# Last expert layer: router in three units, 14 of 16 experts with slots, the shared products behind the slots

## The chip, the cores and the metric

The kernel runs on one core of one Trainium2 chip. The metric is the device time of one execution in microseconds, from the chip's own clock; four runs of the kernel before give 1216.45, 1203.67, 1218.26 and 1219.77 us, a median of 1217.36 us. A further execution was recorded by the hardware profiler. Engines: PE (TensorE, matrix products), DVE (VectorE), ACT (ScalarE), POOL (GpSimd), SP (SyncE, which here only issues DMAs).

## The reference, cut to what matters

Four layers over 1024 tokens of width 256, each wrapped as `x = x + layernorm(layer(layernorm(x)))`: an attention, an expert layer with 8 experts, a linear attention, and an expert layer with 16 experts. Only the last layer is touched:

```python
scores = softmax(x @ gate_weight.T)                  # 1024 x 16
topk_weight, topk_idx = top_k(scores, 4)
for e in range(16):
    w_e = sum(where(topk_idx == e, topk_weight, 0), -1)
    y = y + w_e[:, None] * glu(x, gate_up_weights[e], down_weights[e])   # 176 hidden channels
y = y + glu(x, shared_gate_up, shared_down)          # 352 hidden channels
glu(x, gu, d) = (silu(x @ g.T) * (x @ u.T)) @ d.T
```

Each token needs 4 of the 16 experts. With the inputs of the reference the experts 0 to 13 get between 231 and 290 tokens each.

## The kernel before, in words

Tokens stand in 8 tiles of 128 (`TT`), in two halves of 4 tiles. `self.hT` holds the normalised input by channel, `self.hrow` by token, and `self.x` the residual. The last layer (`experts1`) splits the hidden channels in two kinds.

**For all tokens ("dense").** The 352 shared channels and those of the experts from `SP1` = 13 on (3 x 176) are 880 hidden channels, or 7 tiles of at most 128 (`tiles`, `group(0)` 4 of them, `group(1)` 3). `gates(i, hf)` makes the gate and up product of one tile for one half of the tokens (4 matmuls of 512 columns each in the profile's counts, `gated`, L821 to L824), and leaves silu(g)*u in `mids[hf]`. Channels of routed experts are then multiplied by the router's share per token (`weighted`, L1667). Those shares come from `spreads`: PE turns the router's weights (L1598), ACT copies them (`wT`, L1599), SP writes them to DRAM (L807) and reads them back spread over the partitions (L1609). `self.down(ps, products(hf), ...)` (L837) is the third product, 7 pieces by 4 token tiles for a half.

**By slots.** For experts 0 to 12 every token row is sent to the expert's region of a DRAM tensor `slots` (room for 336 rows each). `routed(hf)` does it for a half of the tokens in two steps: first the logits `pl` (L1500), softmax, the four best, `counts` (L1505 to L1531); then the places by running counts `pr` (L1538 to L1544), `place` (L1556) and 16 indirect DMAs on POOL's queue (L1562), four for each token tile. A branch on whether an expert overflows (`crowded`, `full`) then picks `to_slots`. It fetches an expert's rows (`xs`, L1704, on SP), turns them (L1711), makes the products (L1690), the third product (L1743), scales by share (`ys`, L1748) and adds the rows into one of two DRAM tensors `sums` with three indirect DMAs on POOL (L1753). The experts' weights come three experts at a time (`sw`, L1459, on SP). Last, `sums` are fetched (L1795), added to the dense part, normalised and stored (`turn_out`).

The order of the work is written out by hand in `experts1` for the dense part and the router; a scheduling layer then orders each engine's queue from that program order by its own estimates, and each engine runs its queue strictly in order. The branch is a border: what stands before it in the program is issued before it on every engine. Before it stand all `gates`, `shifted()` (eight ACT additions to `x`, L314), `weighted(0)`, the third product of the first half, and `weighted(1)`; the third product of the second half stands at the end of `to_slots`. While the router runs, the tile pairs of the layer before are still being normalised and turned (`turning`, L276, L277; `catch_up` releases the pieces).

Of the kernel before, what the change touches and what calls it, by code (L numbers as in the profile page):

```python
# [9 lines left out]
F32, I32, U32 = mybir.dt.float32, mybir.dt.int32, mybir.dt.uint32  # L10
AF = mybir.ActivationFunctionType
# [4 lines left out]
P = 128  # L16
T = 1024
TT = T // P
# [14 lines left out]
FS = 2 * F1  # L33


SP1 = 13
CP, CT = 112, 3
CAP = CP * CT
SLOTS = SP1 * T
SPARE = 16 * T  # L40
FD = FS + (E1 - SP1) * F1
FG1 = 4
L1F = [(lo, min(FG1 * P, FD - lo)) for lo in range(0, FD, FG1 * P)]
FT = F1 - P
UP = 64
# [16 lines left out]
class Net:  # L62
# [240 lines left out]
    def shifted(self):  # L303

        nc = self.nc
        lost = self.small.tile([P, 3, TT], F32, tag="lost", bufs=1, name="lost")
        shift = self.small.tile([P, TT], F32, tag="shift", bufs=1, name="shift")
        nc.gpsimd.tensor_tensor(lost, self.mvs[:, :, :, 0], self.rss, ALU.mult)
        nc.gpsimd.tensor_tensor(shift, lost[:, 0, :], lost[:, 1, :], ALU.add)
        nc.gpsimd.tensor_tensor(shift, shift, lost[:, 2, :], ALU.add)  # L310
        nc.gpsimd.tensor_scalar(shift, shift, -1.0, None, ALU.mult)
        for tt in range(TT):
            x = self.x[:, tt, :]
            self.pinned(nc.scalar.activation(x, x, AF.Identity, bias=shift[:, tt : tt + 1]))  # L314

    def catch_up(self, ps, n):

# [1115 lines left out]
    def experts1(self):  # L1433
        nc, tc, a = self.nc, self.tc, self.a
        with ExitStack() as ctx:
# [45 lines left out]
            nc.gpsimd.memset(within, 1.0)  # L1481
            nc.gpsimd.memset(within[:, :, 0:1], 0.0)
            place = one.tile([P, TT, TOP1], I32, name="place")
            counts = one.tile([P, 2, E1], F32, name="counts")

            def routed(hf):

                n = slice(hf * TT // 2, (hf + 1) * TT // 2)
                N = TT // 2
                sh = [P, N, E1]  # L1490

                def new(name, *shape):
                    return small.tile([P, N, *shape], F32, tag=name, name=name)

                v, c = w[:, n, :], chosen[:, n, :]
                pl = ps.tile(sh, F32, tag="b1", name="pl")
                for i in range(N):
                    for k in range(KC):
                        at = (hf * N + i) * P
                        nc.tensor.matmul(  # L1500
                            pl[:, i, :], self.hT[:, k, at : at + P], wr[:, k, :],
                            start=(k == 0), stop=(k == KC - 1),
                        )
# [9 lines left out]
                for i in range(N):  # L1513
# [15 lines left out]
                )  # L1529
                nc.vector.tensor_tensor(v[:, :, SP1:], v[:, :, SP1:], c[:, :, SP1:], ALU.mult)  # L1530
                nc.vector.tensor_reduce(  # L1531
                    counts[:, hf, :], c.rearrange("p t e -> p e t"), AX.X, ALU.add
                )
                yield


                pr = ps.tile(sh, F32, tag="b1", name="pr")
                nc.tensor.matmul(pr, self.earlier, c, start=True, stop=False)  # L1538
                if hf == 1:
                    nc.tensor.matmul(  # L1540
                        pr, self.ones, counts[:, 0:1, :].to_broadcast(sh), start=False, stop=False
                    )
                for i in range(1, N):
                    nc.tensor.matmul(  # L1544
# [13 lines left out]
                )  # L1558
                for i in range(N):
                    for j in range(TOP1):  # L1560
                        tt = hf * N + i
                        sent = nc.gpsimd.indirect_dma_start(  # L1562
                            out=self.slots[:, :],
                            out_offset=bass.IndirectOffsetOnAxis(
                                ap=place[:, tt, j : j + 1].bitcast(U32), axis=0
                            ),
                            in_=self.hrow[:, tt, :], in_offset=None,
                            bounds_check=SLOTS - 1, oob_is_err=False,
                        )
                        tc.declare_no_dep(sent.ins, group="sent", reason="no two tokens share a slot")  # L1570
                        tc.add_to_no_dep_group("sent", sent.ins)
                yield

            def crowded():

                pc = ps.tile([P, E1], F32, tag="b1", name="pc")
                for hf in range(2):
                    nc.tensor.matmul(pc, self.ones, counts[:, hf, :], start=(hf == 0), stop=(hf == 1))
                most = one.tile([P, 1], F32, name="most")
                nc.vector.tensor_reduce(most, pc[:, 0:SP1], AX.X, ALU.max)  # L1580
                over = one.tile([P, 1], I32, name="over")
                nc.vector.tensor_scalar(over, most, float(CAP), None, ALU.is_gt)
                return nc.values_load(
                    over[0:1, 0:1], min_val=0, max_val=1,
                    skip_runtime_bounds_check_because="the result of a comparison",
                )
# [44 lines left out]
            def gates(i, hf, part=None):  # L1631
                wg, wu, right, m, lo = tiles[i]
                self.gated(ps, tmp, wg, wu, mids[hf][0:m, i, :], m, hf, part)

            quarters = (slice(0, HALF // 2), slice(HALF // 2, HALF))
            first, second = (routed(hf) for hf in range(2))
            early, late = quarters
            gates(0, 0, early)
            gates(1, 0, early)
            self.catch_up(ps, 3)  # L1640
            gates(2, 0, early)
            next(first)
            gates(3, 0, early)
            for i in range(FG1):
                gates(i, 0, late)
            self.catch_up(ps, len(self.todo))
            next(first)
            group(1)
            gates(FG1, 0)
            next(second)  # L1650
            for i in range(FG1 + 1, len(tiles)):
                gates(i, 0)
            gates(0, 1)
            next(second)
            gates(1, 1)
            spreads()
            gates(2, 1)
            full = crowded()
            for i in range(3, len(tiles)):
                gates(i, 1)  # L1660
            self.shifted()

            def weighted(hf):
                for i, (wg, wu, right, m, lo) in enumerate(tiles):
                    if lo in spread:
                        v = mids[hf][0:m, i, :]
                        nc.vector.tensor_tensor(  # L1667
                            v, v, spread[lo][0:m, hf * HALF : (hf + 1) * HALF], ALU.mult
                        )

            def products(hf):
                return [(mids[hf][0:m, i, :], right) for i, (wg, wu, right, m, lo) in enumerate(tiles)]

            weighted(0)
            self.down(ps, products(0), True, 0)
            weighted(1)


            def silu_times(g, pg, pu, mid):
# [19 lines left out]
            def to_slots():  # L1699
# [74 lines left out]
                for e in range(SP1):  # L1774
                    if e + 1 < SP1:
                        turn(e + 1)
                    if e + 3 < SP1:
                        fetch(e + 3)
                    middle(e)
                    if e > 0:  # L1780
                        out(e - 1)
                    if e > 0 and e % S3 == 0 and (e // S3 + 1) * S3 < SP1:
                        load(e // S3 + 1)
                out(SP1 - 1)
# [21 lines left out]
                def plus(dst, x, y):  # L1806
                    nc.vector.tensor_tensor(dst, x, y, ALU.add)

                acc = self.acc
                for tts in pairs[:2]:  # L1810
                    plus(acc[:, tts, :], acc[:, tts, :], other[:, tts, :])
                for tts in pairs[:2]:
                    plus(acc[:, tts, :], acc[:, tts, :], got[:, tts, :])
                    self.turn_out(ps, [tts.start, tts.start + 1])
# [2 lines left out]
                self.down(ps, products(1), True, 1, lambda ps, tts: self.turn_out(ps, tts), other)  # L1817

            def to_all():
                self.down(ps, products(1), True, 1)  # L1820
# [119 lines left out]
```

## Time and profile before

| | us |
|---|---|
| median of four runs | 1217.36 |
| profiled execution, own time | 1224.1 |
| its span, first to last instruction | 1222.3 |
| PE busy / DVE / ACT / POOL in the span | 1126.5 / 706.4 / 514.3 / 220.3 |
| last layer, first gate (1003.3) to the end | 219 |
| of it, dense gates and router, to the end of the last gate (1081.5) | 78.2 |
| slots, first `pe` to last `po` (1101.8 to 1188.4) | 86.6 |
| from there to the end | 33.9 |

Read the profile by stage: the layers before the last are the same instructions in both kernels. In what follows a time such as 1101.8 is in microseconds from the start of the span, and "L1690" is line 1690 of the kernel before. The chain of waits lists, in order of time, what the end of the program is traced back to; the timeline lists one engine's instructions with the idle time before them and what ended it. "Another core or an unknown queue" means that the trace has no instruction that fits the release.

### The profile page before, as it was taken

The numbers are of one execution on the slowest core, as the hardware profiler recorded it, in microseconds if no ns is written. First come the engines' busy times: TensorE is split into PE (matmuls) and PEld (weight loads), VectorE is DVE, ScalarE is ACT, GpSimd is POOL, SyncE is SP. The second block draws the span as 40 slices with busy tenths as digits, with TensorE's granted clock in tenths as the row PEclk, the third lists the DMA queues.
The fourth block names the chain that finished last, engine by engine and source line by source line (L and its number), as shares of the span: only waits on it lengthen the run. The fifth ranks groups of instructions, "written<-read, shape, count | busy, mean of one in ns | idle before, by whom it ended". The sixth has DMA issues, their size and how long they took to land. (4 is left out here: it accounts for less than half of the span.)

```text
span 1222.3 us, 15788 instructions
## 1 busy us (share of the span) xinstructions
PE 1126.5 (92%) x5996; PEld 687.4 (56%) x5996; DVE 706.4 (58%) x1664; ACT 514.3 (42%) x970; POOL 220.3 (18%) x208
## 2 busy tenths in 40 slices
PE   7999999998999999789999999999999889589992
PEld 4543333332547465456767676767676666257672
DVE  5876777760434336677677777777777765033224
ACT  4266666667330102355444444444444434023331
POOL 3100000000100001021111111111111224604662
PEclk9999999999999999899999999999999989879997
DMA  6000000000005111201304131313130211285743
GB/s 204 2 1 1 1 1 1 1 1 1 1 8 182 52 37 50 73 11 58 122 26 128 29 125 30 124 32 106 32 105 35 65 39 37 81 220 136 184 64 113
DMA packets 53495, 76.96 MB, mean 63 GB/s; under 512 B 7226, under 2 KB 44409, under 8 KB 53415
## 3 DMA queue, kind: packets, MB, share of 16 engines
q1 hardware_dynamic: 46886, 68.97, 18.4%
q0 software_dynamic: 6528, 6.93, 3.1%
q8 instruction: 49, 0.80, 0.3%
q14 instruction: 32, 0.25, 0.1%
HBM read 60.88 MB, written 17.00 MB: 64 GB/s over the span
## 5 line engine op out<-in xcount | busy, mean ns | idle before, releaser
L499 DVE TENSOR_REDUCE pm<-sc 128x1 f32<-128x512 f32 x256 | 163.2, 685 | 64.4 <-PE sc L563 43.2
L563 PE MATMUL sc<-qTm,kT 32*128 32x512 f32 x512 | 151.7, 646 | 1.9 <-ACT pe L581 1.9
L592 ACT ACTIVATE pe<-sc 128x512 f32<-128x512 f32 x216 | 117.7, 595 | 67.9 <-PE sc L563 47.3
L1144 ACT ACTIVATE sn<-pt,shift,rs 128x128 f32<-128x128 f32 x256 | 93.7, 470 | 106.9 <-DVE shift L1140 106.9
L494 PE MATMUL sc<-kT,qT 32*128 32x512 f32 x512 | 136.2, 637 | 1.6 <-ACT qT L453 0.8
L1104 PE MATMUL px<-hT,w_l1a 128*128 128x512 f32 x256 | 125.4, 602 | 5.4 <-DVE y L1096 5.1
L1096 DVE SCALAR_TENSOR_TENSOR y<-px,cp,y 128x1023 f32<-128x1023 f32 (+5 forms) x102 | 123.4, 1213 | 4.2 <-ACT y L1090 4.1
L1139 POOL TENSOR_TENSOR rs<-ve,nhalf 128x8 f32<-128x8 f32 x32 | 52.4, 1637 | 304.5 <-DVE ve L1138 249.7
L824 DVE TENSOR_TENSOR mid<-sg,pu 128x512 f32<-128x512 f32 (+2 forms) x50 | 32.0, 642 | 122.1 <-PE pu L821 87.3
L823 ACT ACTIVATE sg<-pg 128x512 f32<-128x512 f32 (+2 forms) x50 | 27.6, 561 | 138.4 <-PE pg L821 122.9
L230 POOL TENSOR_TENSOR rss<-ve,nhalf 128x2 f32<-128x2 f32 x12 | 8.4, 698 | 406.5 <-DVE ve L229 401.7
L550 PE MATMUL po<-pe,va 128*32 128x256 f32 (+1 forms) x872 | 79.2, 431 | 1.3 <-ACT oT L555 0.8
L563 PEld LDWEIGHTS sc<-qTm,kT 32*128 32x128 f32 x512 | 49.6, 185 | 54.0 <-issue 38.3
L1208 PE MATMUL pg<-hT,w_l1a 128*128 128x512 f32 x128 | 62.0, 609 | 9.7 <-DVE og L1324 8.2
L1753 POOL DMA_INDIRECT sums<-ys,number x39 | 56.9, 1459 | 72.5 <-ACT ys L1748 64.2
L550 PEld LDWEIGHTS po<-pe,va 128*32 128x32 f32 x872 | 17.8, 108 | 85.3 <-issue 75.7
L1104 PEld LDWEIGHTS px<-hT,w_l1a 128*128 128x128 f32 x256 | 44.2, 196 | 32.7 <-issue 30.8
L821 PE MATMUL pg<-hT,w_l0f 128*128 128x512 f32 x128 | 62.1, 608 | 0.0
L1174 PE MATMUL pv<-w_l1a,hT 128*128 128x256 f32 x256 | 59.9, 382 | 1.3 <-DVE state L1308 0.7
L1114 ACT ACTIVATE y<-y 128x1024 f32<-128x1024 f32 x32 | 34.2, 1068 | 62.7 <-DVE y L1096 54.2
L821 PE MATMUL pu<-hT,w_l0f 128*128 128x512 f32 x128 | 60.3, 592 | 0.0
L1125 DVE BATCH_NORM_STATS2 st<-pt 128x6 f32<-128x128 f32 x256 | 55.1, 283 | 5.3 <-PE pt L1123 5.3
(275 smaller groups left out, 2041.3 us busy)
## 6 DMA issues: line engine op xcount, KB each, us to landing
spread<-rows SPq DMA_DIRECT2D x32, 512.0 KB
sw<-in_e_s SPq DMA_DIRECT2D x4, 1872.0 KB
slots<-blank SPq DMA_DIRECT2D x13, 357.0 KB
xs<-slots SPq DMA_DIRECT2D x13, 357.0 KB
w<-w SPq DMA_DIRECT2D x9, 512.0 KB
w_l0f<-in_e_wg SPq DMA_DIRECT2D x4, 512.0 KB
w_l0f<-in_e_wu SPq DMA_DIRECT2D x4, 512.0 KB
w_l0f<-in_e_wd SPq DMA_DIRECT2D x4, 512.0 KB
```

The lines of the kernel that those rows point to most:

```text
L494: nc.tensor.matmul(sc, raw[r, tt * P : (tt + 1) * P], kT[r, g, half(kh)], start=True, stop=True,)
L499: nc.vector.tensor_reduce(pm[:, tt, 2 * pair + i, kh : kh + 1], sc, AX.X, ALU.max)
L550: nc.tensor.matmul(po[0][rows(j), c], va[:, st, g * G + j, :], pe[j // 2][:, j % 2, c], start=(st == 0), stop=(st == TT - 1 and c.stop == ...
L563: nc.tensor.matmul(sc, kT[rows(j), g, st * P : (st + 1) * P], qm[rows(j), :], start=True, stop=True,)
L592: nc.scalar.activation(pe[pair][:, i, :], sc, AF.Exp, scale=scale)
L821: nc.tensor.matmul(p, w(k), self.hT[:, k, c], start=(k == 0), stop=(k == KC - 1))
L1096: nc.vector.scalar_tensor_tensor(y[:, at:hi], px[:, at - j : hi - j], column(cw + 4 * h + 3 - j), y[:, at:hi], ALU.mult, ALU.add,)
L1104: nc.tensor.matmul(px[:, c], w[:, k, hh * DK : (hh + 1) * DK], self.hT[:, k, c], start=(k == 0), stop=(k == KC - 1),)
L1144: nc.scalar.activation(sn[:, n, :], pts[n // 4][:, n % 4, :], AF.Identity, scale=rs[:, n : n + 1], bias=shift[:, n : n + 1],)
L1174: nc.tensor.matmul(pv[:, i, :, :].rearrange("p h v -> p (h v)"), self.hT[:, k, (n + i) * P : (n + i + 1) * P], wv[:, k, :], start=(k == 0) ...
L1208: nc.tensor.matmul(pg, wg[:, k, hh * DK : (hh + 1) * DK], self.hT[:, k, c], start=(k == 0), stop=(k == KC - 1),)
L1753: sent = nc.gpsimd.indirect_dma_start(out=self.sums[e % 2][:, :], out_offset=bass.IndirectOffsetOnAxis(ap=number[:, i, :].bitcast(U32), axis=0
```

## The change

Three things change in the last layer. `SP1` goes from 13 to 14, so that the dense hidden channels go from 880 to 704 (6 tiles, the last of 64) and `to_slots` runs over 14 experts. The router works in three units (`UNITS`): token tiles 0 and 1, tiles 2 and 3, tiles 4 to 7; the logits of the first unit stand ahead of all dense gates. `weighted` of both halves, the additions of `shifted` and the third product of the first half move behind the branch: `weighted` and the additions into the first experts of `to_slots`, the third product behind the last expert, where it takes the fetched `sums` as its addend.

```diff
-SP1 = 13
+SP1 = 14
+UNITS = ((0, 2), (2, 2), (4, 4))
@@ shifted
-        for tt in range(TT):
+        def add(tt):
             x = self.x[:, tt, :]
-            self.pinned(nc.scalar.activation(x, x, AF.Identity, bias=shift[:, tt : tt + 1]))
+            nc.scalar.activation(x, x, AF.Identity, bias=shift[:, tt : tt + 1])
+        return add
@@ routed
-            def routed(hf):
-                n = slice(hf * TT // 2, (hf + 1) * TT // 2)
-                N = TT // 2
+            def routed(u):
+                begin, N = UNITS[u]
+                n = slice(begin, begin + N)
...
-                if hf == 1:
+                for i in range(u):
                     nc.tensor.matmul(
-                        pr, self.ones, counts[:, 0:1, :].to_broadcast(sh), start=False, stop=False
+                        pr, self.ones, counts[:, i : i + 1, :].to_broadcast(sh), start=False, stop=False
                     )
@@ order of the work
-            first, second = (routed(hf) for hf in range(2))
+            units = [routed(u) for u in range(len(UNITS))]
             early, late = quarters
+            next(units[0])
             gates(0, 0, early)
+            self.catch_up(ps, 3)
             gates(1, 0, early)
-            self.catch_up(ps, 3)
+            next(units[1])
             gates(2, 0, early)
-            next(first)
+            next(units[0])
             gates(3, 0, early)
-            for i in range(FG1):
+            gates(0, 0, late)
+            next(units[1])
+            for i in range(1, FG1):
                 gates(i, 0, late)
             self.catch_up(ps, len(self.todo))
-            next(first)
             group(1)
             gates(FG1, 0)
-            next(second)
+            next(units[2])
             for i in range(FG1 + 1, len(tiles)):
                 gates(i, 0)
             gates(0, 1)
-            next(second)
+            next(units[2])
             gates(1, 1)
             spreads()
             gates(2, 1)
             full = crowded()
             for i in range(3, len(tiles)):
                 gates(i, 1)
-            self.shifted()
+            shift = self.shifted()
...
-            weighted(0)
-            self.down(ps, products(0), True, 0)
-            weighted(1)
@@ to_slots
                     if e > 0:
                         out(e - 1)
+                    if e in (3, 4):
+                        weighted(e - 3)
+                    if 0 <= e - 3 < TT:
+                        shift(e - 3)
...
                 acc = self.acc
-                for tts in pairs[:2]:
-                    plus(acc[:, tts, :], acc[:, tts, :], other[:, tts, :])
+                self.down(ps, products(0), True, 0, None, other)
                 for tts in pairs[:2]:
                     plus(acc[:, tts, :], acc[:, tts, :], got[:, tts, :])
                     self.turn_out(ps, [tts.start, tts.start + 1])
```

More of the change, by code (lines that the diff above doesn't have):

```diff
@@ L305, in shifted @@
         nc = self.nc
-        lost = self.small.tile([P, 3, TT], F32, tag="lost", bufs=1, name="lost")
-        shift = self.small.tile([P, TT], F32, tag="shift", bufs=1, name="shift")
+        lost = self.route.tile([P, 3, TT], F32, name="lost")
+        shift = self.route.tile([P, TT], F32, name="shift")
         nc.gpsimd.tensor_tensor(lost, self.mvs[:, :, :, 0], self.rss, ALU.mult)
@@ L1483, in experts1 @@
             place = one.tile([P, TT, TOP1], I32, name="place")
-            counts = one.tile([P, 2, E1], F32, name="counts")
-            def routed(hf):
-                n = slice(hf * TT // 2, (hf + 1) * TT // 2)
-                N = TT // 2
+            counts = one.tile([P, len(UNITS), E1], F32, name="counts")
+            def routed(u):
+                begin, N = UNITS[u]
+                n = slice(begin, begin + N)
                 sh = [P, N, E1]
                 def new(name, *shape):
-                    return small.tile([P, N, *shape], F32, tag=name, name=name)
+                    return small.tile([P, TT // 2, *shape], F32, tag=name, name=name)[:, 0:N]
                 v, c = w[:, n, :], chosen[:, n, :]
@@ L1498, in routed @@
                     for k in range(KC):
-                        at = (hf * N + i) * P
+                        at = (begin + i) * P
                         nc.tensor.matmul(
@@ L1531, in routed @@
                 nc.vector.tensor_reduce(
-                    counts[:, hf, :], c.rearrange("p t e -> p e t"), AX.X, ALU.add
+                    counts[:, u, :], c.rearrange("p t e -> p e t"), AX.X, ALU.add
                 )
@@ L1560, in routed @@
                     for j in range(TOP1):
-                        tt = hf * N + i
+                        tt = begin + i
                         sent = nc.gpsimd.indirect_dma_start(
@@ L1576, in crowded @@
                 pc = ps.tile([P, E1], F32, tag="b1", name="pc")
-                for hf in range(2):
-                    nc.tensor.matmul(pc, self.ones, counts[:, hf, :], start=(hf == 0), stop=(hf == 1))
+                for u in range(len(UNITS)):
+                    nc.tensor.matmul(
+                        pc, self.ones, counts[:, u, :], start=(u == 0), stop=(u == len(UNITS) - 1)
+                    )
                 most = one.tile([P, 1], F32, name="most")
@@ L1819, in to_all @@
             def to_all():
-                self.down(ps, products(1), True, 1)
+                for tt in range(TT):
+                    shift(tt)
+                for hf in range(2):
+                    weighted(hf)
+                    self.down(ps, products(hf), True, hf)
                 for e in range(SP1):
```

## The prediction

> **What bounds the kernel now.** Up to 1001 the two kernels run the same instructions, so only the last layer counts. I read its stages first (busy time by stretch), then the chain of waits, then the timelines of POOL, PE and DVE. The stretches show PE full from 1010 to 1050 and from 1101 to 1201, and between them a hole: from 1050 to 1070 PE is busy 5.8 of 20 us, DVE 0.7, ACT 1.2, while POOL works. The chain of waits goes through it:
>
> ```profile
> 1037.35 0.04 ACT sg L823
> 1037.39 14.40 another core or an unknown queue
> ...
> 1052.41 16.95 another core or an unknown queue
> ...
> 1069.38 0.57 ACT wT L1599
> ...
> 1071.40 1.57 DMA w<-wT
> ...
> 1074.34 8.12 DMA w<-w
> ...
> 1082.52 18.76 DMA sw<-in_e_s
> ...
> 1101.81 0.55 PE pe L1690
> ```
>
> Read it as: the router's shares reach ACT at 1069.4, are written and spread by DMA, the experts' rows and weights queue behind them, and the slots start at S = 1101.8. The first 31 us have no owner. By PE's timeline its work was done in time: the turn of the shares (L1598) ends at 1044.4, yet ACT copies it at 1069.4; a gate product ends at 1041.8 and ACT takes it at 1051.8. PE's completions arrive 5 to 25 us late, one in some 8 us, and then all the backlog within 0.4 us at 1070.8. It lies beside POOL's sends:
>
> ```profile
> 1025.38 1.24 POOL L1562 DMA_INDIRECT slots<-hrow,place  x1 [8.97 <-DVE place L1556]
> ...
> 1065.83 0.98 POOL L1562 DMA_INDIRECT slots<-hrow,place  x1 [0.30 <-issue]
> ```
>
> 32 sends, one each 1.28 us, end at 1066.8; the backlog comes 4.0 us later. From 1025 to 1039 they ran without any such delay. The profile shows where it lies, not why. From S on PE sets the pace:
>
> ```profile
> 1088.27 12.02 PE L837 MATMUL po<-w_l1f,mid 112*128 112x256 f32 x44 [0.66 <-DVE mid L1667]
> ...
> 1112.45 3.57 PE L1690 MATMUL pe<-xT,sw 128*128 128x336 f32 x12
> ...
> 1119.03 3.57 PE L1690 MATMUL pe<-xT,sw 128*128 128x336 f32 x12
> ...
> 1188.36 12.27 PE L837 MATMUL po<-w_l1f,mid 128*128 128x256 f32 x56
> ```
>
> One expert takes 1119.03 - 1112.45 = 6.58. The last third products (56) hide behind the last experts' sums, whose fetch lands at 1203.1 to 1205.1; the end is DVE's.
>
> **The change, part by part.** Let S be the start of the slots and compare with 1101.8.
>
> *The extra expert.* +6.58 us of PE from S on. Its three sends on POOL are 3 x 1.76 = 5.3, below 6.58, and its weights ride with the last load (two experts for one): nothing more. Its blank rows are one more DMA of 357 KB in the linear attention, where the DMA share is 1 to 3 tenths: 0.
>
> *The smaller dense part.* 7 tiles to 6. A tile costs 3.43 per half (pg to pg), also at 112 rows, so the gates lose 6.9 us of PE; third products lose 8 of 56 per half, 3.4. This is worth only what S gets from it, counted there. SP issues five spreads for seven, 1.4 MB for 2.2.
>
> *Third product of the first half behind the slots.* PE has 96 matmuls after the last expert for 56: 96 x 0.215 = 20.6, to 1209.0 on the old clock. DVE adds the sums at 1203 or later anyway, and takes the last pair's product at 1211.6 before. So PE stays covered. But DVE's queue comes out otherwise: in the kernel before the pairs of tiles overlap (while one waits for POOL's power, the next pair's statistics run); in the built order after, each pair runs through alone. From rows: addition 0.65, sums 0.65 (two pairs only), statistics 0.75, aggregates 0.2, eps 0.1, POOL 0.85, nb 0.16, then 1.6 to the second `x`. First pair: sums land 1203.1, then 0.65 + 0.75 + 0.2, two additions to `hrow` that wait for later fetches (to about 1207.5), nb and `x`: 1209.2. Second 5.0: 1214.2. Two more of 4.3: 1222.8. Before, the last `x` ends at 1217.3: +5.5; with some overlap left I take +5.0 (bounds 0 and +6).
>
> *Shares and additions behind the branch.* In the built order DVE's eight multiplications (5.5 us) and ACT's additions (7 x 0.41) stand in front of the first rows' copies. They wait for spreads that land before the rows, since both go through SP's queue: 0 while S waits for the weights, up to +5.5 if not.
>
> *PE idles before S.* Its gates end, and nothing is left until the rows land. A row for a cold start: after 1000 the first gate pieces of 256 columns took 1.87, 1.70 and 1.17 for 0.87: 2.1 us lost. I take +2.0 (bounds 0 and 3). Before, the third products stood there and half filled the gap.
>
> *The router in three units.* First sends: PE's logits of unit 0 end near 1004.6, but DVE interleaves its router steps with the last normalisations, ACT needs a table load (1.28) and stands `hT` of the second pair behind the third pair's rows. Counting DVE's rows in the built order, the place of unit 0 comes near 1018 (before: 1024.5), unit 1 near 1024. So the first 16 sends run 1018.7 to 1039.2. In exchange PE waits in its queue for pair two's `hT` (2.0), for `pr` of unit 0 (0.5) and unit 1 (3.0), and starts gates(4) near 1028.5 instead of 1023.2. Then gates 3.43, logits 1.7, gates 3.43, gates 3.43: `pr` of unit 2 at 1040.5 to 1041.7, its place at 1043. POOL has stopped by then; 16 sends take 0.9 + 20.5, to 1064.4. Six us won in front shrink to 2.4 at the end of the sends.
>
> *Sends beside DVE.* The new first burst (1018.7 to 1039.2) overlaps DVE's last normalisations and router steps. The row: from 1024 to 1039 DVE was busy 5.7 of 15 us and the sends kept their 1.28 all the same. So 0; the other bound is 4 sends that take the 1.76 of a sending in the slots: +1.9, inside POOL's pause.
>
> The Trainium skill speaks against it ("SBUF — State Buffer", "SBUF: two separate sides", the box on the "DVE blocks DMA" trap): while DVE runs an operation that takes the port it shares with GpSimd, POOL cannot write descriptors, and a send of 0.62 us takes 3.1. By that rule, as an estimate from the page, five sends beside DVE would each be 2.5 us longer, the first burst would end at 1051 and S come some 8 us later; the pace of 1.28 above shows nothing of it for the operations DVE runs here.
>
> *S.* SP's first `xs` waits for the last send, and the weights stand behind it in SP's queue. Landing +1.0 after the last send (packets of the trace end near 1067.8), then rows and first weights, 2.3 MB at 0.36 MB/us (the best stretch while `sw` runs alone) plus 2.4 for issue and receipt: +8.8. So S = place of unit 2 + 31.2. The other path is the shares: from ACT's copy, 2.9 to the first spread, 1.4 + 2.3 MB at the 0.24 MB/us seen from 1074 to 1092, 18.3 in all. The dense third product, which PE held until 1100.1, isn't in either.
>
> **Sum.** Own time after = 1224.1 + (S - 1101.8) + 6.6 + 5.0 + 2.0 = S + 135.9. Break-even is S = 1088.2. If no completion came late, S = 1043 + 31.2 = 1074.2, 1210.1. If some do in the first 16 sends, and go out while POOL stands still, unit 2's place slips to about 1049 (the first late one cost DVE 4.7 at 1040), the shares get out in the first 14 us of the second burst as at 1025 to 1039, and S = 1080: 1215.9, -8.2. The timed runs have a median of 1217.36, 0.55% below the profiled execution; the same difference there gives **1209**.
>
> **Rivals.** *The hole is back whole*: late completions last to 4 us after the sends, in the second burst too. Place near 1047.7, sends to 1069, shares at 1073.1 to 1074.8, S = 1093.1: +4.9, **1222**. For it: the shares are turned at 1045, inside the second burst. Against: a pause of 4 us or more lets the backlog go. *No late completions*: -14, **1203**. For it: bursts of 16 instead of 32, and 14 us without delay at the start of the old one; against: nothing in the change aims at the cause, which is unknown. *Slower*: the place of unit 2 is the late thing. Three units mean that four results of PE (`pl` and `pr` of units 1 and 2) stand on the path to it instead of two, each 5 to 10 late if completions are late from the first burst on: 1043 + 26 = 1069, S = 1100, +12, **1230**. It is slower at all from a place at 1057 on, and by 1% from 1069. For it: POOL now waits for a place three times, and the old trouble began at 1039 within a microsecond of POOL's long wait for its second place (1038.4 to 1045.9); against: POOL pauses also between units. *It doesn't do what it says* (the first place is no earlier than 1024): no price, since unit 2 decides.
>
> **Chances.** Forecast 0.40 (1203 to 1216), no late completions 0.25 (1199 to 1206), hole back 0.18 (1216 to 1226), slower 0.17 (1226 to 1234). A measurement of this kernel tells about 1% from no change. Below 1205.2 lie most of the second case and a quarter of the first: 0.32; over 1229.5 the last and a little: 0.18; between, 0.50. The range is 1199 to 1228: what is left out is the slow end of the last rival and the tail of the second.
>
> **What would show it.** Right: two bursts of 16 sends with a pause near 1040, `wT` more than 15 us before 1069, first `pe` at 1074 to 1088 ended by `sw` or `xs`, 6.58 per expert, PE done about 21 us after its last `po` of an expert, DVE's last `x` some 34 after it, for 28.9 before. Wrong: releases without an owner after the second burst, a place of unit 2 after 1057, slots that wait for DVE's multiplications, or a tail that PE ends.

## The result

After: median 1216.24 us of 44 runs (1213.30 to 1221.27). Before, now with 70 runs: 1216.02 us (1201.35 to 1225.53). The ratio after to before is 1.0028, 95% interval [1.0014, 1.0042]: 0.3% slower, which lies within the 1% that counts as no change; 1209 was forecast. The ratio leaves out runs over 1.5% above the fastest of their kernel, 21 of before's 70 and none of after's; the profiled execution of before (1224.1) would be one of them. The medians of all runs are 0.2 us apart, so the kernels are equally fast on the whole. The two ranges say more than the medians: before spreads over 24 us, after over 8.

The profiled execution of after took 1217.18 us of its own (span 1215.4). The chain of waits of after, to be read beside that of before:

```profile
1063.01 3.08 PE pg L825 x4
1066.13 0.98 another core or an unknown queue
...
1068.70 2.31 DMA slots<-hrow,place
...
1071.96 8.42 DMA xs<-slots
1080.52 1.35 PE pt L1716 x6
1081.87 5.22 PE pe L1695 x12
```

The 31 us without an owner are one microsecond, and the slots start at S = 1081.7 instead of 1101.8. They now wait for the last send and the fetch behind it. POOL's timeline of after has the two bursts of 16 sends and the pause between them, here the ends of each:

```profile
1017.18 1.24 POOL L1566 DMA_INDIRECT slots<-hrow,place  x1 [2.33 <-DVE place L1560]
...
1036.60 0.97 POOL L1566 DMA_INDIRECT slots<-hrow,place  x1 [0.30 <-issue]
1049.54 0.97 POOL L1566 DMA_INDIRECT slots<-hrow,place  x1 [11.96 <-issue]
...
1068.70 0.97 POOL L1566 DMA_INDIRECT slots<-hrow,place  x1 [0.30 <-issue]
```

Late completions are still there, but cut short; late means that the engine that waits for PE's result goes on well over 0.1 us after PE has ended it. PE's timeline of after at the end of the second burst, and ACT's, which takes these gate products:

```profile
1055.90 1.96 PE L825 MATMUL pg<-hT,w_l1f 128*128 128x512 f32 x4
...
1059.42 1.88 PE L825 MATMUL pg<-hT,w_l1f 128*128 128x512 f32 x4
...
1062.94 1.93 PE L825 MATMUL pg<-hT,w_l1f 128*64 128x512 f32 x4
```

```profile
1058.29 0.60 ACT L827 ACTIVATE sg<-pg 128x512 f32<-128x512 f32 x1 [3.90 <-PE pg L825]
1066.11 0.60 ACT L827 ACTIVATE sg<-pg 128x512 f32<-128x512 f32 x1 [7.23 <-PE pg L825]
1072.47 0.59 ACT L827 ACTIVATE sg<-pg 64x512 f32<-64x512 f32 x1 [5.76 <-remote]
```

The three gate products ended at 1057.9, 1061.3 and 1064.9, so ACT got them 0.4, 4.8 and 7.6 us late, the second with three sends still to go and the third 2.8 us after POOL's end (1069.7). The first burst shows the same from 1030 to 1040: the gate product that ended at 1032.4 was taken at 1040.0.

So the slots gain 20.1 us between the two profiles. What is given back: first product to last third product of the experts 94.3 us for 86.7, and from there to DVE's last sum 34.2 for 28.8. -20.1 + 7.6 + 5.4 and 0.2 at the end is -6.9, the difference of the two profiled executions.

### The profile page after: what moved, and what is told of

Read it like the earlier page. It is cut to its first block, busy times and chain, and to the rows that moved or that the text cites. A ratio compares the mean times of both kernels' runs of the same rounds, so it can differ in the third digit from the quotient of the medians.

```text
span 1215.4 us, 15834 instructions
## 1 busy us (share of the span) xinstructions
PE 1127.6 (93%) x6000; PEld 688.0 (57%) x6000; DVE 706.7 (58%) x1683; ACT 517.2 (43%) x975; POOL 225.0 (19%) x211
## 5 line engine op out<-in xcount | busy, mean ns | idle before, releaser
L1758 POOL DMA_INDIRECT sums<-ys,number x42 | 61.5, 1464 | 52.5 <-ACT ys L1753 43.6
L1118 ACT ACTIVATE y<-y 128x1024 f32<-128x1024 f32 x32 | 34.2, 1067 | 62.7 <-DVE y L1100 54.3
```

The costliest lines, as they stand in the source:

```text
L1758: sent = nc.gpsimd.indirect_dma_start(out=self.sums[e % 2][:, :], out_offset=bass.IndirectOffsetOnAxis(ap=number[:, i, :].bitcast(U32), axis=0
```

## The experiments

S is the start of the slots, "tail" the time from the last third product of an expert to DVE's last sum. In each comparison the kernel before was run too, on the same chip; its median stands with it, because it turned out to matter. The second and the third comparison were taken on one chip, the first, fourth and fifth on one each.

**First comparison (before: 1202.53, 1199.68 to 1204.38 in 18 runs).** The kernel before again, and each part of the change alone.

Before, unchanged:

> The kernel before, unchanged, profiled a second time. Theory V (the late completions of PE beside POOL's sends last a different time in each execution, and the one profiled first had a long hole): own time anywhere from 1201 to 1225, the start of the slots S moves with it one for one (own time = S + 122 within 2), S comes 31 to 33 us after the last late copy of the shares, and the 32 sends keep their pace of 1.28 us. Rival P (the profile itself makes the hole, the timed executions have none): again 1222 to 1226, S again 1100 to 1104, and the hole from 1050 to 1070 is back in the same place.

Measured: own time 1201.68, S = 1078.1. ACT's timeline of this execution:

```profile
1042.81 1.05 ACT L1599 COPY wT<-pt 3x512 f32<-3x512 f32 x2 [1.56 <-PE pt L1598]
1044.96 0.60 ACT L823 ACTIVATE sg<-pg 128x512 f32<-128x512 f32 x1 [1.10 <-PE pg L821]
1048.84 0.60 ACT L823 ACTIVATE sg<-pg 128x512 f32<-128x512 f32 x1 [3.28 <-PE pg L821]
```

The same instructions as in the profile shown with the forecast, and the same 32 sends of 1.28 us, but the shares are copied at 1042.8 instead of 1069.4 and from 1032 on every gate product is taken within 0.1 us of PE's end. The hole isn't in the kernel; it is in some executions of it. A lower clock isn't the difference: up to 1000 both profiles have a granted clock of 0.98 to 1.00 in every stretch of 200 us, and at the router's first place they are 1.2 us apart. Without the hole S is 23.7 us earlier and the execution 22.4 us shorter. Its chain of waits shows what sets S then:

```profile
1065.05 2.22 DMA slots<-hrow,place
...
1068.23 9.03 DMA xs<-slots
...
1078.34 4.92 PE pe L1690 x12
```

The last send, and the rows behind it: the same that set it in after, where S is 3.5 us later.

The 14th expert alone:

```diff
-SP1 = 13
+SP1 = 14
```

> The kernel before with 14 instead of 13 experts by slots and nothing else. Theory V: the dense part loses 10 us of PE work ahead of the slots, but the slots wait for shares and sends, not for PE, so nothing of it comes back: +6.6 us, median about 1222 to 1223, ratio 1.004 to 1.007. Rival E (PE's work ahead of the slots sets S in the timed executions): -10 + 6.6, median 1212 to 1214, ratio 0.996 to 0.998.

Measured: ratio 1.0062 [1.0042, 1.0082], +6.7 us between the medians; S 1078.4, unmoved though the gates ended 6.1 us earlier. As the first theory had it: the shorter dense part buys nothing.

The router in three units alone, with 13 experts and the rest of the work back in its place (main lines of the edit against the kernel after):

```diff
-SP1 = 14
+SP1 = 13
...
+            weighted(0)
+            self.down(ps, products(0), True, 0)
+            weighted(1)
...
-                self.down(ps, products(0), True, 0, None, other)
```

> The kernel after with 13 experts by slots and with the multiplications by the shares, the additions of the shift and the third product of the first half back ahead of the branch: of the change only the router in three units is left. Theory V: the shares reach ACT near 1052 as in the kernel after, PE ends its gates near 1069 and the third product near 1081, the last send ends near 1069, S = 1081 to 1085, own time = S + 122.3 = 1203 to 1207, ratio 0.988 to 0.994. Rival P (no hole outside the profile): S is 1 to 5 us earlier than in the timed executions of the kernel before at most, ratio 0.996 to 1.002. Rival W (the third product waits for the spreads, as it did from 1081 to 1100 in the kernel before): S 1090 or later, ratio 0.998 to 1.004.

Measured: 0.9983 [0.9973, 0.9993]. That is the number of rival P and not of theory V, but it doesn't decide between them: before had no execution with a hole on this chip, so there was none to remove. The last send is not earlier (1067.2 for 1066.0): the first starts 5.7 us earlier, and POOL then stands still for 7 us until the third unit has its places.

Products, multiplications and additions behind the branch alone (main lines, against the kernel before):

```diff
-            weighted(0)
-            self.down(ps, products(0), True, 0)
-            weighted(1)
...
+                self.down(ps, products(0), True, 0, None, other)
```

> The kernel before with the third product of the first half, the multiplications by the shares and the additions of the shift moved behind the branch, as in the kernel after; 13 experts by slots, router in two halves. Theory V: shares as late as before, S 0 to 2 us earlier, and the tail from the last send of sums to the end 5 to 7 us longer (33.2 in the kernel after, 26.1 before): median 1219 to 1223, ratio 1.003 to 1.007. Rival E (PE's work ahead of the slots sets S): third product of 12 us gone from the path, tail +7: ratio 0.993 to 0.997.

Measured: 1.0045 [1.003, 1.0061], +5.5 us; S 1079.4, the tail 36.1 for 29.1. The three parts add to 6.7 - 2.4 + 5.5 = +9.8 us.

**Second comparison (before: 1213.01, 1202.67 to 1221.68 in 35 runs).**

After, unchanged:

> The kernel after, unchanged, on the chip of this comparison. Theory C (whether PE's completions come late is a matter of the chip or the execution, not of the kernel; without late ones the start of the slots S is 1078 before and 1075 to 1080 after, and the change then only pays: 6.6 for the expert and 7 for the tail): if the kernel before has a median near 1202 here, this one has 1211 to 1216, ratio 1.008 to 1.012; if it has 1212 or more, this one has 1214 to 1220, ratio 0.994 to 1.004. Rival R (the change is worth the same everywhere): ratio 1.001 to 1.005 whatever the median of before.

Measured: 1.0034 [1.0008, 1.006], median 1214.69, S = 1081.9, late completions as in the first profile of after. Within what the theory gave for such a chip; the rival had the same number here.

After with 13 experts (`SP1 = 13`):

> The kernel after with 13 experts by slots instead of 14, all else as after. Theory C: 6.6 us of PE less from S on, S as in the kernel after (the last send sets it; the gates end 5 to 7 us later, about 1066 to 1070, still ahead of it): 6 to 7 us below the kernel after of the same chip, and 5 to 7 above the router in three units alone (the tail). Rival E (PE's gates set S): only 0 to 3 below the kernel after.

Measured: 0.9975 [0.9946, 1.0003], 5.5 us below after, a little less than expected; S 1079.1.

Before with the weights' load ahead of the rows:

```diff
-                fetch(0)
                 load(0)
+                fetch(0)
```

> The kernel before with one line moved: the load of the first three experts' weights stands ahead of the fetch of the first expert's rows on SP, so that it runs while the last sends do. Theory Q (SP's queue sets S: the rows wait for the last send and the weights stand behind them): the weights land before the last send, S moves from 1078 to 1072 to 1074, -4 to -6 us, ratio 0.995 to 0.997. Rival E (the third product, which ends near 1073, or the rows set S): 0 to -2. Rival B (the weights' 1.9 MB slow the last sends): the last send is later than 1067 and S no earlier, 0 to +3.

Measured: 0.9994 [0.995, 1.0038]. Its profiled execution has a hole (shares at 1058.6 and 1064.2, S = 1091.7), so the question wasn't answered. Eight of its ten runs lie between 1212 and 1215.3, two at 1198.1 and 1198.4: by these times the hole is there or not, in one kernel on one chip. The two short ones lie 4 us below the shortest of before's 35 (1202.7), which is what theory Q gives without a hole; with two runs and no profile of them that isn't shown.

After with four differences (main lines), with which the sends were to run without a pause (in the tail, `dense` adds a pair's third product, `last_sum` the fetched sums, `measure` and `scaled` are the two halves of the normalisation, `store` adds to `x`; the instructions are kept in this order):

```diff
+            gates(1, 0, late)
+            self.catch_up(ps, len(self.todo))
+            next(units[2])
+            for i in range(2, FG1):
+                gates(i, 0, late)
+            next(units[2])
+            group(1)
+            gates(FG1, 0)
...
+                load(0)
                 fetch(0)
...
+                last_sum(acc, 1)
+                measure(1)
+                scaled(0)
+                last_sum(other, 2)
+                dense(2)
+                store(0)
+                measure(2)
+                scaled(1)
```

> The kernel after with four differences: 13 experts by slots; the logits and the places of the third unit directly behind those of the second, so that POOL's sends run without a pause; the weights' load ahead of the first fetch of rows; and the tail's instructions on DVE written so that the next pair of tiles is added and measured while POOL and ACT work on the last. Theory C: sends from 1017 to 1059, S 1065 to 1068, 87 to the last third product of an expert, 29 to 31 from there: own time 1184 to 1190, on a chip where the kernel before has 1202: ratio 0.986 to 0.990. Rival E (PE's gates end near 1067 and set S): S 1068 to 1070, ratio 0.990 to 0.992. Rival T (the tail is bound by the products behind the slots, 24 us of PE, and by the fetches, not by DVE's order): tail 34 to 36, ratio 0.992 to 0.998.

Measured: 1.0029 [1.0001, 1.0058], and none of the forecasts for S: 1092.3. The third unit's logits ended on PE at 1025.5, but a gate product ahead of its next steps on ACT's and DVE's queues, which had ended at 1027.8, was taken at 1040.3, 12.5 us later, 1.3 of them a table load. The place came at 1045.7, PE stood still for 13 us meanwhile, and the gates ended at 1083. Starting sends earlier had put the router itself behind the late completions. The tail was 30.2: that part worked.

**Third comparison (before: 1213.56, 1204.11 to 1220.16 in 28 runs): what makes PE's completions late.**

A fill on POOL behind every send:

```diff
+                        self.pinned(sent)
+                        self.pinned(nc.gpsimd.memset(idle, 0.0))
```

> The kernel before with a fill of 128 x 384 values on POOL behind every send, which serves nothing but time: the 32 sends come each 1.7 to 1.9 us instead of each 1.28, about the pace of the sends of sums in the slots, and end near 1080. Theory D (PE's completions come late because the sends come faster than something drains them, so that it fills after some 10): no completion late by more than 2 us, place of the second half before 1042, shares at ACT before 1046, S = 1091 to 1096 set by the last send, times within 3 us of each other. Rival N (a fixed time of 10 to 14 us after the burst begins, whatever the pace): late completions from 1036 on until 3 to 4 us after the last send, S 1110 or later, if the kernel before is above 1210 on this chip. On a chip where the kernel before is near 1202 no completion is late either way, and the run only prices the sends: S 1091 to 1096.

Measured: 0.9981 [0.9943, 1.0018], 1205.7 to 1213.3. POOL's timeline has the new pace, 1.57 us from send to send, and ACT's has the shares in time:

```profile
1028.02 0.97 POOL L1563 DMA_INDIRECT slots<-hrow,place  x1 [0.17 <-issue]
1028.99 0.43 POOL L1574 MEMSET idle<- 128x384 f32 x1
1029.59 0.98 POOL L1563 DMA_INDIRECT slots<-hrow,place  x1 [0.17 <-issue]
```

```profile
1043.18 1.05 ACT L1602 COPY wT<-pt 3x512 f32<-3x512 f32 x2 [1.55 <-PE pu L821]
```

No gate product is taken more than 0.1 us late from 1030 on, through 50 us of sends. S = 1088.0 is set by the last send (1074.8), both earlier than expected since a fill takes 0.44; the ten times still spread over 7.5 us, where 3 were expected, for 16 of before. Ten of before's 28 times in this comparison lie below 1208, so one profile without late completions could still be chance; the fifth comparison has more.

The second half's sends left out:

```diff
-                for i in range(N):
+                for i in range(N if hf == 0 else 0):
```

> The kernel before without the 16 sends of the second half; the slots of those tokens stay blank and their routed part is left out. Theory D: late completions, if the chip has them, only from about 1037 to 3 us after the 16th send, near 1048; then all in time; shares at ACT by 1050 and S = 1073 to 1078, set by PE's gates, the third product and the weights. Rival X (the sends are not the cause, only near in time): a hole of 15 us or more is still there, up to 1065 to 1070.

Measured: 1191.17 in two runs. ACT's timeline:

```profile
1045.61 0.60 ACT L823 ACTIVATE sg<-pg 128x512 f32<-128x512 f32 x1 [10.37 <-PE pc L1578]
1046.10 1.03 ACT L1599 COPY wT<-pt 3x512 f32<-3x512 f32 x2
...
1050.76 0.60 ACT L823 ACTIVATE sg<-pg 128x512 f32<-128x512 f32 x1 [2.66 <-PE pg L821]
```

PE's completions of 1039 to 1045 arrive together at 1045.6 to 1045.9, 2.5 us after the last send (1043.1), and then in time; S = 1072.9. Sends gone, hole gone.

32 sends of 64 bytes a row:

```diff
-                            out=self.slots[:, :],
+                            out=self.narrow[:, :],
...
-                            in_=self.hrow[:, tt, :], in_offset=None,
+                            in_=self.hrow[:, tt, 0:16], in_offset=None,
```

> The kernel before with all 32 sends, but each of 16 values for a token (64 bytes) instead of 272, to another DRAM tensor; the slots stay blank, so the routed part is left out, and the fetch of rows waits for no send. Theory D with descriptors (what fills is counted in rows sent, not in bytes): late completions as in the kernel before, 10 to 25 us of them, where that has them. Rival Y (bytes): 17 times fewer bytes, no completion late by more than 2 us.

Measured: 1195.8 to 1217.4 in 8 runs. ACT's timeline of the profiled one:

```profile
1063.16 0.57 ACT L1600 COPY wT<-pt 3x512 f32<-3x512 f32 x1 [12.13 <-remote]
1069.46 0.58 ACT L1600 COPY wT<-pt 3x512 f32<-3x512 f32 x1 [5.73 <-remote]
```

In the first profile of before the two copies start at 1069.4 and 1070.8. So the hole is there with a seventeenth of the bytes, and ends about as late: it isn't the bytes that count. Whether it is the rows or the sends no run tells, since every send had 128 rows.

After with 13 experts and the interleaved tail:

> The kernel after with 13 experts by slots and with the tail's instructions on DVE written so that the next pair of tiles is added and measured while POOL and ACT work on the last one; router in three units, products behind the slots. S as with 13 experts and the old tail (1079 on the chip where that was 1209.2), the tail from the last third product of an expert to the last sum 30 instead of 35.6: 5 to 6 us below that, 1203 to 1204, where the kernel before has 1213 (ratio 0.991 to 0.994); 1200 to 1203 where the kernel before has 1202 (ratio 0.998 to 1.001). Rival T (the tail's gain goes to the fetches): ratio 0.996 to 1.0.

Measured: 1203.11, ratio 0.9919 [0.9885, 0.9953]. DVE's timeline of after shows the old tail, one pair of tiles at a time:

```profile
1199.62 0.16 DVE L203 SCALAR_TENSOR_TENSOR nb<-mv,rs 128x2 f32<-128x2 f32 x1 [0.81 <-POOL rs L202]
1200.45 0.92 DVE L338 TENSOR_TENSOR x<-x,acc 128x256 f32<-128x256 f32 x2 [0.67 <-ACT acc L335]
1201.28 0.68 DVE L847 TENSOR_TENSOR acc<-hrow,po 128x512 f32<-128x512 f32 x1
```

Twice in each pair DVE waits, 0.8 for POOL's power and 0.7 for ACT's scaling. In this kernel other pairs' work stands in those places, and the same steps of the first two pairs wait for nothing (its DVE timeline); the last two pairs still wait 0.7 each for ACT:

```profile
1184.99 0.15 DVE L1850 SCALAR_TENSOR_TENSOR nb<-mv,rs 128x2 f32<-128x2 f32 x1
1185.07 0.69 DVE L1831 TENSOR_TENSOR hrow<-hrow,hT 128x512 f32<-128x512 f32 x1
...
1186.46 0.75 DVE L1861 TENSOR_TENSOR x<-x,acc 128x256 f32<-128x256 f32 x2
```

Tail 30.2, where it was 35.6 with 13 experts and the old order.

**Fourth comparison (before: 1200.94, 1198.00 to 1204.17 in 29 runs).** No late completion in any of the four profiles.

> The router in three units alone (13 experts by slots; multiplications, additions and third product of the first half ahead of the branch), measured again beside the whole change. Theory D, where the kernel before has a median above 1210: the pause of POOL between the second and the third unit lets the late completions go, the second burst's cost 5 to 9 us of PE at the end of the gates; gates end 1068 to 1072, third product 12 us later, S = 1082 to 1086, own time 1204 to 1209, ratio 0.990 to 0.995. Rival N (units as such gain nothing): ratio 0.998 to 1.001. Where the kernel before is near 1202: ratio 0.998 as already measured.

The router alone: 0.9990 [0.9981, 0.9999]. Its chain of waits shows the next limit, PE without a gap:

```profile
1063.16 1.72 PE pu L825 x4
1064.88 12.10 PE po L841 x56
1076.98 1.05 PE pt L1721 x9
```

> The kernel after, unchanged, for the comparison with the router alone. Theory D: the expert's 6.6 and the tail's 5 to 7 stand on top of the router alone, less 2 to 4 that its shorter gates win back: 1213 to 1217 on any chip; ratio 0.998 to 1.004 where the kernel before is above 1210, 1.008 to 1.012 where it is near 1202. Rival M (the parts don't add): less than 5 above the router alone.

The whole change: 1.0076 [1.0061, 1.0091], +9.7 us between the medians, the sum of its parts in the first comparison (+9.8). S = 1076.3, place of the third unit 1042.8.

> The kernel with all four differences (13 experts by slots, third unit directly behind the second, weights ahead of the rows, tail interleaved) and with a fill of 128 x 320 values on POOL behind every send, so that one takes 1.52 us. Theory D: no completion late, place of the third unit before 1042, sends from 1017 to 1067, gates end near 1067, S = 1072 to 1077, own time 1193 to 1198 on every chip. Rival N (not the pace; without it the same kernel had 1214.9): the third unit's place again near 1046 and the gates' end after 1080, 1210 or later.

> As the one with a fill behind every send, but with a fill behind every second one, so that a send takes 1.40 us on average. Theory D, limit below 1.40: no late completions, sends from 1017 to 1062, gates end near 1067, S = 1069 to 1074, own time 1190 to 1195. Limit above 1.40: completions late from later in the burst than in the kernel before (after some 20 sends or more instead of 11), gates end 1070 to 1080, S = 1075 to 1085, own time 1197 to 1207.

The kernels with four differences and a fill behind each send or each second one: 0.9989 [0.9980, 0.9997] and 0.9999 [0.9989, 1.0009], medians of 1200.1 and 1201.7 where theory D, with nothing late, had 1193 to 1198 and 1190 to 1195. S was 1079.7 and 1074.6, later than expected: PE stood still for 2.3 us before the third unit's places, so that the gates ended at 1072.7 and 1069.4, and in the first, with the weights' load beside the last sends, the packets of the last one took 5.8 us after it, for 2.2 in before. Where the limit lies between 1.28 and 1.52 us was not told, since nothing was late here at any pace.

**Fifth comparison (before: 1220.13, 1215.71 to 1224.32 in 11 runs).**

> The kernel with all four differences and a fill behind every send (1.52 us for one), again. Theory D: 1197 to 1203 whatever the kernel before has; where that is above 1210, ratio 0.986 to 0.992, no completion late by more than 2 us between 1030 and 1070, place of the third unit before 1040. Rival N: 1210 or later where the kernel before is above 1210, as the same kernel without the fills (1214.9).

> The kernel after with 13 experts by slots and the interleaved tail, again. Theory D: where the kernel before is near 1202, S as in the kernel after there (1076 to 1079) and the tail 30: 1196 to 1201, ratio 0.996 to 1.0; where that is above 1210, 1203 again (ratio 0.990 to 0.994), 2 to 5 above the paced kernel. Rival T (the tail's gain is lost where PE is early): ratio 1.002 to 1.005 near 1202.

The paced kernel: 1200.62, ratio 0.9851 [0.9823, 0.9878]; unpaced with 13 experts and the interleaved tail: 1203.92, 0.9868 [0.9843, 0.9893]. Both times are where the first theory put them; the ratios are a little lower because before was slower here than in the third comparison. ACT's timeline of the paced one, well inside its sends (1019 to 1067):

```profile
1052.01 1.05 ACT L1608 COPY wT<-pt 3x512 f32<-3x512 f32 x2 [1.56 <-PE pt L1607]
1054.17 0.60 ACT L827 ACTIVATE sg<-pg 128x512 f32<-128x512 f32 x1 [1.10 <-PE pg L825]
```

Nothing late at 1.52 us, on a chip where the kernel before lost most. The unpaced kernel of this comparison, with its sends at 1.28, has late completions: gate products that PE ended at 1063.5 and 1066.9 are taken by ACT at

```profile
1067.28 0.60 ACT L827 ACTIVATE sg<-pg 128x512 f32<-128x512 f32 x1 [5.77 <-issue]
1072.27 1.09 ACT L827 ACTIVATE sg<-pg 128x512 f32<-128x512 f32 x2 [4.39 <-PE pu L825]
```

The same holds for all ten profiles with sends at 1.28 us from the chips where before has its long times (second, third and fifth comparison and the two profiles of the result); the two paced ones from there have none. The paced kernel has 1200.1 and 1200.6 where before has 1200.9 and 1220.1. It is the version that beats both: before by 1.5% where completions are late and by 0.1% where not, after by 10.6 us in the fourth comparison.

## Why the prediction was wrong

**Its walk through the change held.** Place of the third unit 1049 (measured 1048.8), two bursts with a pause, S = 1080 (1081.7); with the measured S the sum S + 135.9 gives 1217.6 (profiled: 1217.18). The likeliest case, with late completions in the first 16 sends that go out in the pause and no second hole, is what the trace shows. The slip of 6 us at the third place was right in size partly by luck: it was taken from a late result of the router itself (4.7 in before), and in after it was a gate product, taken at 1040.0 instead of 1032.4, that stood ahead of the router's steps on ACT and DVE.

**The step that failed is the conversion:** "the timed runs have a median of 1217.36 us, 0.55% below the profiled execution; the same difference there gives 1209". It took the hole of one execution, S = 1101.8, for a property of the kernel, and the 0.55% for something that the profiler adds. After's profiled execution lies 0.08% above its median. Before's lay high because its hole was long. The forecast's own sum for after was 1215.9, and the median of before is 1216.0: set beside each other, they say no change, which is what was measured. The case without late completions shows the same: its sum was 1210.1, converted to 1203, and where nothing was late after had 1210.6 (fourth comparison). The four times of before had the clue: 1203.67 beside three between 1216 and 1220. The later profile without a hole (1201.68) says what that run most likely was; its price belonged into the forecast as a second case, in which the change costs 10 us instead of gaining 7.

**Terms of the sum.** The extra expert +6.6: +6.7 alone. Tail +5.0: 5.4 between the two profiles, 7.0 with 13 experts alone; the reason given, each pair running through alone, is in DVE's waits above. Cold PE +2.0: the experts took 94.3 us in after for 86.7 in before, so the term measures +1.0 beside the expert's 6.6; where PE ran into the slots without a gap (router alone, 85.6) or with one (before without a hole, 87.6) the difference is 2.0. The end of the sends to S, 1.0 + 8.8: 12.0 to 12.6, so the forecast had 2 to 3 too little (the last packets land 2.3 after the start of the last send, the rows are 8.4 to 9.1 in flight); this is most of why S came 1.7 late although the third place was right. PE's 96 matmuls behind the last expert, 20.6: 23.8, still ahead of DVE. Multiplications ahead of the first rows, 0: DVE ended them at 1078.9, before the last rows that S waited for (1080.4). No late completions in after, S = 1074.2: 1076.3, with the place at 1042.8 for 1043.

**Rivals.** "The hole is back whole" and "slower, since the third unit's place is late" did not occur in after. The second did in the kernel with the sends brought forward, where it cost 13 us of PE. What the forecast gave in its support, a long wait of POOL from 1038.4 to 1045.9, isn't in POOL's timeline of before: the sends run on there at 1.28 us, and the only gap is 0.75 us before 1046.6. "No late completions" did occur, but on both kernels at once, where it favours before. That the sends beside DVE would slow down by the Trainium skill ("SBUF — State Buffer", "SBUF: two separate sides") was not seen: the first burst of after runs beside DVE's router steps and gate products (DVE busy for 4.9 of 21 us; the last normalisations end before it) and keeps 1.28. No run shows which of these operations take the port of which the page speaks.

**Unsettled.** Why some chips or executions have late completions was not found: two comparisons had no time of before above 1204.4 in 47 runs; in the other three 53 of 74 lie above 1211, which is read from times and from the profiles of the kernels run beside them. That PE's completions come late with sends at 1.28 us each and not with a fill behind each (1.52 or more) is shown by two kernels on two chips; that it is the pace, and not the fill as such, between two sends is argued, since no run slowed the sends in another way. Through which part of the chip PE's completions wait for POOL is not known.

## What to carry to other kernels

Before pricing a change against one profile, ask whether that execution is typical: one run 13 us away from three others, or a wait with no owner, can mean that the baseline itself has more than one time, and the forecast then needs one sum for each. When an engine's results arrive late beside a dense run of indirect sends, pace the sends before rearranging the work. A pace has its price: 0.29 us more for each moved S by 10 us in the kernel before, which came out no faster (ratio 0.9981 [0.9943, 1.0018]), and a pace of 1.52 by under 2 where the sends start 6 us earlier and run without a pause. In a tail that alternates between engines, write the next tile's additions and statistics into the gaps: that took 5.4 us off this tail.

## What the runs showed of the hardware

Indirect sends of 128 rows, one each 1.28 us, made PE's completions late from about the 9th to the 12th send of a burst (1030.7 and 1059.6 in after, 1039 in before) until 2.4 to 4.0 us after the last, on some chips and, by the times, in most executions there. DVE's and ACT's completions came in time: in the midst of before's sends ACT's of 1052.4 and DVE's of 1061.7 released PE within 0.1 us. With 32 sends without a pause about one completion of PE in 8 us came through (taken at 1044.7, 1051.8, 1061.0 and 1069.4 in before). The effect was there with rows of 64 instead of 1088 bytes too, and absent with a fill behind each send, at 1.52 and 1.57 us a send. The Trainium skill ("DMA: Bandwidth & Descriptors", "SWDGE vs HWDGE vs iDMA") says that GpSimd builds descriptors for such transfers and appends them to rings before any byte moves, which would fit an effect that doesn't go by bytes; no run here shows this building of descriptors, and that sends can hold up another engine's completions is shown by the runs alone.
